# Seven sets of sixteen sequences in the seven-product form instead of five, and the rest in one group of eight, one of two and two of four

## The chip, the cores and the metric

The kernel runs on one core of a Trainium2 chip. Five engines work side by side, each through its own list of instructions in order: TensorE (PE in the profile; PEld is its weight load), VectorE (DVE), ScalarE (ACT), GpSimd (POOL) and SyncE (SP), whose list mostly issues transfers. The metric is device time in microseconds, the median of several runs.

## The reference

There are 128 sequences of 64 tokens with 256 features. Every token goes through two shared networks, and through one of five experts, which a label of its sequence chooses; a small gate on the first token of each sequence weighs the three outputs. The sum is added to x, and a diffusion step over tokens and features follows.

```python
s0 = _dense(x, swi[0], swo[0])                 # relu(x @ wi) @ wo, 256 -> 1024 -> 256
s1 = _dense(x, swi[1], swo[1])
h  = relu(einsum('bsd,bdf->bsf', x, wi[type_label]))
eo = einsum('bsf,bfd->bsd', h, wo[type_label])
w  = softmax(relu(concat(eo[:,0], s0[:,0], s1[:,0]) @ g1) @ g2)
x  = x + eo * w[:,0] + s0 * w[:,1] + s1 * w[:,2]
x  = x + (zX * lap_x + zY * lap_y + zR * x * (1 - x))
```

The labels are drawn from 0, 1 and 2 alone. In the drawn inputs 43 sequences have label 0, 50 have label 1 and 35 have label 2. The kernel learns this only on the chip.

## The kernel before

**Precision.** Every operand of a product is kept as a high and a low part (`split`, L121: ScalarE rounds the value into the high part, another engine, mostly VectorE, subtracts to get the low part). One product is then three matmuls: high by high, high by low, low by high. In the second layer "wide" matmuls of 512 columns hold the high and the low part of the output weights side by side, and "narrow" ones of 256 columns add the low part of the hidden layer.

**Units and slots.** `order_batches` (L261) counts the labels, gives every sequence a slot, and writes a small integer table `tab`: which sequence sits in which slot, which expert each unit of four slots (`NB`) has, and one last number that decides a branch. An expert's sequences are first laid out in sets of sixteen (four units), then the rest of it in pairs of units, then single full units, then what is less than three sequences. `base` holds the ends of these stretches; `base[5]` is the number of slots in sets of sixteen, `base[10]` that in sets of sixteen and pairs. This is a chain of small VectorE operations, called in three pieces behind the second shared item.

**Stages.** The program is one fixed list:

1. Two shared items on the first 1024 tokens (n = 0, 1), which also split the shared weights and store the split parts in DRAM, as `wo_d` (for the second layer) and `wi_d` (for the first).
2. `NQUAD` = 5 items of the expert on units 0 to 19 (n = 100 to 104), one set of sixteen sequences each.
3. `stream` (L1128): nine groups on the rest: pairs of units (8 sequences, 512 columns), among them a half group (two sequences), then single units (4 sequences, 256 columns): units 20-21, 22-23, 24-25, the half group at unit 32, 26-27, 28, 29, 30, 31.
4. A branch (`tc.If`, L1271): if the last number of `tab` is over 128, units 32 to 34 are worked too, each as a single group. The body lies in the program between this place and the next stage; every engine jumps over it or runs through it.
5. The shared items n = 2 to 31 on the other tokens, with the gate (`load_gate`, `gate_shared`, `gate_hidden_s`, ... in n = 2), the sum and the diffusion.

**Items and groups.** An item (L847, `unit` L702) works 1024 tokens in the seven-product form: the first layer of a quarter of the features is 7 products in place of 8, from sums of weight blocks and of token blocks. It has 84 matmuls of 512 columns in the first layer, 64 wide and 64 narrow ones in the second. A group is plain: a pair of units has 48 matmuls of 512 columns in the first layer (`up`, L1030), 32 wide and 32 narrow ones in the second (`down`, L1044); a single unit has 48 of 256 columns, 16 wide and 16 narrow. `stream` walks a group in steps of two features: two `up`, then the `down` of the step before. Each `up` is evacuated by ScalarE into `gh` (high) and by VectorE into `gl` (low); `down` waits for these.

**What else stage 3 carries.** `ahead(g, f)` (L1077) hangs other work on each feature of a group: the loads of the next group (`load_group_w` L439: first a register load of the expert, then four transfers of 512 KB; `load_group_x` L408: 64 KB for each sequence) and the splits of its weights (`split_group_w` L467, tiles `gwr` into `gw`; for the half group `hi` and `ho`). The first two quarters of the shared first-layer weights had been used plain (`plain_units`), so `reload(u)` and `again(u)` load them again (`wsr`), add up the blocks on GpSimd (`sum_wi`, tile `wsum`), split them (tile `wi`) and store them (`keep_wi`, the transfer `wi_d<-wi`). The split second-layer weights come back (`load_wo`, eight of 512 KB), the next tokens come in (`load_x(1)`) and are split, and the first two first-layer parts and one row for the gate are loaded.

**Order.** In items the order of every engine is that of the code. In groups, other than the half group and the first step after it, only TensorE and the transfers keep the code's order (`in_order`, L115); the tile scheduler places the work of the other engines in their lists when the program is built. SyncE's list is one queue: a transfer that waits for its source holds back all behind it. Before the branch ends, each engine signals an event that the others may wait for.

At the very start `NWARM` matmuls on a cleared tile run while the first loads are on their way (L246).

Of the kernel before, what the change touches and what calls it, by code (L numbers as in the profile page):

```python
# [12 lines left out]
ALU = mybir.AluOpType  # L13
# [4 lines left out]
B, S, D, F = 128, 64, 256, 1024  # L18
NE = 5
NF = F // P  # L20
NQ = NF // 2
NB = 4
NU = B // NB + NE * (NB - 1) // NB
NSLOT = NU * NB
NQUAD = (B // NB - 3 * NE + 3) // 4
NPAIR = (B // NB - NE + 2) // 2
NBIG = NPAIR - 2 * NQUAD
NSURE = B // NB + 1 - 2 * NPAIR
HALF = NBIG - 1
UH = 2 * NPAIR + NSURE - 1  # L30
GROUPS = [(2 * NB * g, 2 * NB) for g in range(2 * NQUAD, NPAIR)] + [(u * NB, NB) for u in range(2 * NPAIR, UH)]
GROUPS.insert(HALF, (UH * NB, NB // 2))
NRUN = len(GROUPS)
GROUPS += [(u * NB, NB) for u in range(UH, NU)]
NG = len(GROUPS)
ST = 4
NT = S // ST
# [1 line left out]
N = ST * B  # L39
LAG = 2  # L40
EI = 100
NWARM = 8


A11, A12, A22, S1, S2, S3, S4 = range(7)
# [4 lines left out]
def cond_resid_kernel(ctx: ExitStack, tc: tile.TileContext, xg, xs, xn, itok, z, we, ws, g1, g2, out):  # L50
# [192 lines left out]
    vec.memset(idle, 0.0)  # L243
    for i in range(2):
        pw = seeded(f"pm_idle{i}")
        for _ in range(NWARM // 2):  # L246
            mm(pw, idle[:, :P], idle, True, True)
    it_i = const.tile([P, 1], I32, name="it_i")
    nc.gpsimd.dma_start(it_i, itok)
# [11 lines left out]
    def order_batches():  # L261
# [100 lines left out]
            vec.tensor_tensor(ge[0], ge[0], ge[i], ALU.min)  # L362
        vec.tensor_tensor(tab[:, NSLOT : NSLOT + NU], ge[0], ge[3], ALU.min)

        vec.tensor_scalar(gt[:, 0:1], base[0:1, 4 * NE :], float(-NB), None, ALU.add)
        vec.tensor_tensor(tab[:, NSLOT + NU :], gt[:, 0:1], base[0:1, 3 * NE : 3 * NE + 1], ALU.max)
        yield
        pm3 = psum("pm_perm")
        mm(pm3[0:1, 0:NSLOT], bc, own, True, True)
# [38 lines left out]
    def load_group_x(g):  # L408
        s0, n = GROUPS[g]
        xr = gxr[g] = group_tile(g, [P, n, 2 * S], F32, "gxr")  # L410
        load_batches(s0, n, lambda j: xr[:, j, :])
# [27 lines left out]
    def load_group_w(g):  # L439
        group_expert(g)  # L440
        for h in range(NQ):
            r = own(g, ("raw", h), lambda: slot4(f"gwr{g}_{h}", F32))
            dma(r, we[bass.ds(gval[g], 1), :, 2 * h : 2 * h + 2, :].rearrange("o p f c -> p (o f) c"))
            graw[g, "both", h] = r
            graw[g, 2 * h], graw[g, 2 * h + 1] = r[:, 0, :], r[:, 1, :]

    def load_group(g):
        load_group_w(g)
        load_group_x(g)
# [17 lines left out]
    def split_group_w(g, f):  # L467
        w = own(g, ("w", f), lambda: slot4(f"gw{g}_{f}"))
        split(w[:, 0, :], w[:, 1, :], graw[g, f], vec)
        gw[g, f] = w  # L470
# [4 lines left out]
    def split_half_w(f):  # L475

        h = f // 2
        r = graw[HALF, "both", h]
        if f % 2:
            w = hout[h] = slot4(f"ho{h}").rearrange("p h c -> p (h c)").rearrange("p (f h c) -> p f h c", f=2, h=2)  # L480
            split(w[:, :, 0, :], w[:, :, 1, :], r[:, :, 256:512], vec)
        else:
            if h % 2 == 0:
                for part in range(2):
                    t = slot4(f"hi{h // 2}{part}")
                    hin[h // 2, part] = t.rearrange("p h c -> p (h c)").rearrange("p (f c) -> p f c", f=4)
            hi, lo = (hin[h // 2, part][:, h % 2 * 2 : h % 2 * 2 + 2, :] for part in range(2))
            split(hi, lo, r[:, :, 0:256], vec)
# [588 lines left out]
    def ahead(g, f):  # L1077

        if g >= NRUN:
            return  # L1080
        if f == 0:
            if g == NRUN - 3:
                slots = nc.values_load(
                    tab[0:1, NSLOT + NU : NSLOT + NU + 1], min_val=0, max_val=NSLOT,
                    skip_runtime_bounds_check_because="the table's entries are bounded on the chip",
                )
                total.append(slots)
            if g + 1 < NRUN:
                if g <= NBIG and g != HALF:
                    load_group_w(g + 1)  # L1090
                if g != HALF:
                    load_group_x(g + 1)
            if g < 2:
                reload(g)
            for u in range(3 * g, min(3 * g + 3, 2 * NQ)):
                load_wo(u)
            if g == NRUN - 2:
                load_x(1)
            if g == NRUN - 1:
                load_wi(2, 0)  # L1100
                load_wi(2, 1)
                load_row()
        if f == 5 and g < 2:
            again(g)
        if g + 1 == HALF and f == 4:
            load_group_x(g + 2)
        if f == 6 and (g + 1 == HALF or NBIG <= g < NRUN - 2):
            load_group_w(g + 2)
        if g == 0 and f + FIRST < NF:
            split_group_w(0, f + FIRST)  # L1110
        if g == HALF + 1 and f + 4 < NF:
            split_group_w(g, f + 4)
        if g + 1 < NRUN:
            if f == (0 if g == HALF else 4):
                split_group_x(g + 1)
            if g + 1 == HALF:
                split_half_w(f)
            elif g == HALF + 1:
                for k in ((), (), (0,), (1,), (2, 3), (4, 5), (6,), (7,))[f]:
                    split_group_w(g + 1, k)  # L1120
            elif g != HALF or f < 4:
                split_group_w(g + 1, f)
        elif f < 7:
            if f < 4:
                sum_x(1, T1 + f, gps)
            split_x(1, (B11, B21, T2, T3, T1, T4, B22)[f], vec)
# [37 lines left out]
    def at(k, *work):  # L1164

        return {divmod(k, 4): list(work)}
# [39 lines left out]
    def reload(u):  # L1206
        e, q = divmod(u, NQ)
        load_raw(u, ws[e, :, 2 * q : 2 * q + 2, :])

    def again(u):  # L1210

        sum_wi(u, gps)
        split_wi(u)
        keep_wi(u)
        wip.pop(u)
# [114 lines left out]
    for p in range(1, NP):  # L1330
        ta, tb = 2 * p, 2 * p + 1
        for e in range(2):
            n = 2 * p + e
            parts = [ahead_w(n)]
            if n == 2:
                parts.append(at(0, load_gate, gate_shared))
                parts.append(at(1, gate_hidden_s))
                parts.append(at(4, lambda: load_y(0)))
                parts.append(at(5, step_factors))
                parts.append(at(4, gate_expert))  # L1340
                parts.append(at(6, gate_hidden_e, lambda: load_y(2)))
                parts.append(at(7, lambda: load_sh(0)))
                parts.append(at(8, lambda: load_eo(0)))
                parts.append(at(9, lambda: load_y(3)))
                parts.append(at(10, gate_weights))
                parts.append(sums(0, 11))
                parts.append(at(12, lambda: load_eo(2)))
                parts.append(at(13, lambda: load_y(1)))
                parts.append(at(16, lambda: load_sh(1)))
                parts.append(starts(ta, 17, 0))  # L1350
            elif n == 3:
                parts.append(at(0, lambda: load_eo(3), lambda: load_eo(1)))
                parts.append(sums(1, 1))
                parts.append(starts(tb, 5))
                parts.append(diffusion(0, 7, True, 4))
                parts.append(at(12, lambda: halo(1)))
                parts.append(next_x(2))
            elif n == 4:
                parts.append(at(2, lambda: load_y(4)))
                parts.append(diffusion(1, 0, False))  # L1360
                parts.append(at(6, lambda: load_eo(4)))
                parts.append(diffusion(2, 6))
                parts.append(at(9, lambda: load_y(5)))
                parts.append(at(11, lambda: load_eo(5)))
                parts.append(starts(ta, 14))
                parts.append(starts(tb, 16, 0))
            elif e == 0:
                parts.append(at(0, lambda t=ta: load_y(t), lambda t=ta: load_eo(t)))
                parts.append(at(4, lambda t=tb: load_y(t), lambda t=tb: load_eo(t)))
                parts.append(diffusion(ta - 2, 2))  # L1370
                parts.append(starts(ta, 10))
                parts.append(starts(tb, 13))
            else:
                parts.append(diffusion(ta - 1, 2))
                parts.append(next_x(p + 1))
            if n == 2 * NP - 1:
                parts.append(at(4, lambda: load_last(n)))
                parts.append(at(8, lambda: split_last_w(n)))
                parts.append(at(9, lambda: split_last_x(n)))
                parts.append(at(10, diagonal))  # L1380
                parts.append(at(12, lambda: halo(ta)))
            left = item(n, left, join(*parts))
# [38 lines left out]
```

## Time and profile before

| | us |
|---|---|
| median of 3 runs | 1032.73 |
| lowest, highest | 1032.59, 1033.43 |
| the profiled execution | 1033.12 |
| its span | 1031.1 |
| TensorE busy in the span | 1025.0 |
| VectorE busy | 811.7 |
| ScalarE busy | 572.2 |
| GpSimd busy | 155.5 |

The span is the time from the first to the last instruction on the core; the execution's own time is 2.0 us longer. Lines of the timeline give start and length of an instruction, engine, line, operation, output<-input and, in brackets, how long the engine had been idle and who ended it. A length includes the drain: matmuls of 512 columns have 390 ns of length and follow each other every 228 ns. Times are microseconds from the span's start. Line 93 and line 108 are helpers that record every matmul and every operation of the other engines, so the tiles' names tell the work.

### The profile page before, as it was taken

What the parts mean: (1) busy time and instruction counts of PE and PEld (TensorE: products, weight loads), DVE (VectorE), ACT (ScalarE), POOL (GpSimd) and SP (SyncE); (2) the same over time, 40 slices, a digit from 0 to 9 for tenths busy, and PEclk for the clock granted to TensorE, in tenths of its full rate; (3) what the DMA queues carried; (4) which work ended last, traced back from release to release, by engine and by line L of the source; (5) the groups of instructions that cost most, each with busy time, mean ns of one, the idle gap of its engine ahead of it and who ended that gap; (6) DMA issues with size and microseconds to landing.
All of it is one profiled execution on the core that took longest, in us unless ns stands there. A gap on an engine that the chain in (4) does not pass through costs nothing.

```text
span 1031.1 us, 15580 instructions
## 1 busy us (share of the span) xinstructions
PE 1025.0 (99%) x5385; PEld 878.2 (85%) x5385; DVE 811.7 (79%) x1498; ACT 572.2 (55%) x1077; POOL 155.5 (15%) x165
## 2 busy tenths in 40 slices
PE   9999999999999999999999999999999999999998
PEld 6878888888888889988888888888888888888888
DVE  7998987988768577758988778678688688688778
ACT  6466776676656467543653644455455364365363
POOL 3000000000013011211441220212212202022020
PEclk9999999999999999999999999999999999999999
DMA  6477233331458766464435435334344163253321
GB/s 219 174 271 259 71 109 94 103 123 52 134 168 308 263 221 196 164 228 175 165 126 175 167 106 178 123 123 168 120 162 158 63 229 123 82 189 133 128 77 47
DMA packets 67122, 159.13 MB, mean 154 GB/s; under 512 B 7680, under 2 KB 34688, under 8 KB 67040
## 3 DMA queue, kind: packets, MB, share of 16 engines
q1 hardware_dynamic: 64512, 149.46, 42.3%
q0 software_dynamic: 2384, 8.52, 2.5%
q8 instruction: 43, 0.70, 0.3%
q14 instruction: 39, 0.32, 0.1%
q10 hardware_dynamic: 144, 0.13, 0.0%
HBM read 126.75 MB, written 31.33 MB: 153 GB/s over the span
## 4 chain that ended last, share of the span: by engine, by line
PE 55%; DVE 2%; issue 0%; ACT 0%; DVEq 0%; ACTq 0%
PE acc L93 29%; PE pb L93 11%; PE pa L93 7%; PE pd L93 7%; DVE eq L108 1%; PE pu L93 0%; DVE eb L108 0%; DVE yb L108 0%; PE pgs L93 0%; DVE ea L108 0%; PE gacc L93 0%; PE pge L93 0%; ACT eq L108 0%; DVE lq L108 0%; DVE gh L108 0%
## 5 line engine op out<-in xcount | busy, mean ns | idle before, releaser
L93 PE MATMUL pb<-x,wi 128*128 128x512 f32 x729 | 207.2, 392 | 0.1
L108 ACT ACTIVATE u<-pb 128x512 f32<-128x512 f32 x162 | 96.9, 598 | 114.8 <-PE pb L93 112.7
L93 PEld LDWEIGHTS pb<-x,wi 128*128 128x128 f32 x729 | 130.9, 189 | 23.6 <-ACT u L108 1.2
L93 PE MATMUL pd<-x,wi 128*128 128x512 f32 x486 | 137.9, 392 | 0.3
L93 PE MATMUL pa<-x,wi 128*128 128x512 f32 x486 | 137.1, 390 | 0.4 <-DVEq L1271 0.4
L108 ACT ACTIVATE pb<-pa 128x512 f32<-128x512 f32 x81 | 47.2, 583 | 118.1 <-PE pa L93 117.4
L108 DVE SCALAR_TENSOR_TENSOR yb<-acc,wgt,yb 128x256 f32<-128x256 f32 x216 | 99.3, 482 | 16.0 <-PE acc L93 12.2
L93 PEld LDWEIGHTS pd<-x,wi 128*128 128x128 f32 x486 | 90.8, 188 | 22.3 <-DVE c L108 2.4
L93 PEld LDWEIGHTS pa<-x,wi 128*128 128x128 f32 x486 | 89.8, 188 | 18.7 <-DVEq L1271 0.6
L108 DVE TENSOR_TENSOR c<-pd,u 128x512 f32<-128x512 f32 x81 | 55.9, 690 | 43.3 <-ACT u L108 32.4
L108 POOL TENSOR_TENSOR la<-yb 128x508 f32<-128x508 f32 (+1 forms) x28 | 32.1, 1147 | 260.7 <-ACT yb L108 259.1
L93 PE MATMUL up<-gxh,gw 128*128 128x512 f32 (+1 forms) x256 | 67.7, 337 | 0.0
L93 PE MATMUL acc<-wo,h_6b 128*128 128x256 f32 (+1 forms) x172 | 56.7, 334 | 0.0
L93 PE MATMUL acc<-wo,h_1b 128*128 128x256 f32 (+1 forms) x172 | 56.7, 333 | 0.0
L93 PE MATMUL acc<-wo,h_7b 128*128 128x256 f32 (+1 forms) x172 | 56.7, 333 | 0.0
L93 PE MATMUL gacc<-gw,gh 128*128 128x512 f32 (+1 forms) x256 | 56.6, 363 | 0.0
L93 PE MATMUL acc<-wo,h_2b 128*128 128x256 f32 (+1 forms) x172 | 56.6, 333 | 0.0
L93 PE MATMUL acc<-wo,h_3b 128*128 128x256 f32 (+1 forms) x172 | 56.5, 332 | 0.0
L93 PE MATMUL acc<-wo,h_4b 128*128 128x256 f32 (+1 forms) x172 | 56.5, 332 | 0.0
L93 PE MATMUL acc<-wo,h_5b 128*128 128x256 f32 (+1 forms) x172 | 56.5, 332 | 0.0
L93 PE MATMUL acc<-wo,h_0b 128*128 128x256 f32 (+1 forms) x172 | 56.4, 332 | 0.0
L108 DVE TENSOR_TENSOR pd<-pd,u 128x512 f32<-128x512 f32 x81 | 55.8, 689 | 0.7 <-PE pd L93 0.6
(275 smaller groups left out, 2446.9 us busy)
## 6 DMA issues: line engine op xcount, KB each, us to landing
wi<-wi_d SPq DMA_DIRECT2D x55, 896.0 KB, 4.5
gwr<-we_in SPq DMA_DIRECT2D x32, 512.0 KB, 5.0
wsr<-we_in SPq DMA_DIRECT2D x20, 512.0 KB, 5.0
xr<-xs_in SPq DMA_DIRECT2D x32, 256.0 KB, 5.0
yb<-xn_in SPq DMA_DIRECT2D x16, 512.0 KB, 5.7
wi_d<-wi SPq DMA_DIRECT2D x8, 896.0 KB, 4.5
y_out<-lq SPq DMA_DIRECT2D x27, 256.0 KB, 2.0
xr<-xg_in SPq DMA_DIRECT2D x80, 64.0 KB, 2.0
```

The lines of the kernel that those rows point to most:

```text
L93: nc.tensor.matmul(out_ap, lhsT=lhsT, rhs=rhs, start=start, stop=stop, skip_group_check=True)
L108: ins = call(*args, **kwargs)
```

## The change

`NQUAD` becomes 7: units 20 to 27 become two more items in the seven-product form (n = 105, 106). Behind them stand four groups: the pair of units 28 and 29, the half group at unit 32, and the single units 30 and 31. Since other labels may not give seven sets of sixteen and one pair, the branch's number is raised to 140 when `base[5]` is under 112 or `base[10]` under 120, and the branch's body then works units 20 to 29 as single groups too: 13 groups in place of 3. For the drawn labels `base[5]` is 112, `base[10]` is 120 and the number is 128, so the body is jumped over in both kernels.

All the work that `ahead` hung on nine groups now hangs on four: both reloads and the half group's loads at the first feature of the pair, the two `again` at its features 3 and 6, the loads of unit 30 at its feature 4, those of unit 31 at feature 6 of the half group. The register of the branch is loaded at the first group. `NWARM` is 9. In n = 2, `gate_hidden_s` comes one place later in the unit. The compiled body that is jumped over has 289 instructions on VectorE (69 before), 481 on ScalarE (101), 352 on SyncE (81).

```diff
-NQUAD = (B // NB - 3 * NE + 3) // 4
-NPAIR = (B // NB - NE + 2) // 2
-NBIG = NPAIR - 2 * NQUAD
-NSURE = B // NB + 1 - 2 * NPAIR
-HALF = NBIG - 1
-UH = 2 * NPAIR + NSURE - 1
-GROUPS = [(2 * NB * g, 2 * NB) for g in range(2 * NQUAD, NPAIR)] + [(u * NB, NB) for u in range(2 * NPAIR, UH)]
-GROUPS.insert(HALF, (UH * NB, NB // 2))
+NFOUR = (B // NB - 3 * NE + 3) // 4
+NQUAD = NFOUR + 2
+UPAIR = 4 * NQUAD
+UH = B // NB
+HALF = 1
+GROUPS = [(UPAIR * NB, 2 * NB), (UH * NB, NB // 2)] + [(u * NB, NB) for u in range(UPAIR + 2, UH)]
 NRUN = len(GROUPS)
-GROUPS += [(u * NB, NB) for u in range(UH, NU)]
+GROUPS += [(u * NB, NB) for u in (*range(4 * NFOUR, UPAIR + 2), *range(UH, NU))]
...
-NWARM = 8
+NWARM = 9
...
-        vec.tensor_tensor(tab[:, NSLOT + NU :], gt[:, 0:1], base[0:1, 3 * NE : 3 * NE + 1], ALU.max)
+        vec.tensor_tensor(gt[:, 0:1], gt[:, 0:1], base[0:1, 3 * NE : 3 * NE + 1], ALU.max)
+        for i, u in ((1, UPAIR), (2, UPAIR + 2)):
+            few = gt[:, i : i + 1]
+            vec.tensor_scalar(few, base[0:1, i * NE : i * NE + 1], float(u * NB), float(NSLOT), ALU.is_lt, ALU.mult)
+            vec.tensor_tensor(gt[:, 0:1], gt[:, 0:1], few, ALU.max)
+        vec.tensor_copy(tab[:, NSLOT + NU :], gt[:, 0:1])
...
         if f == 0:
-            if g == NRUN - 3:
+            if g == 0:
                 slots = nc.values_load(
...
-            if g + 1 < NRUN:
-                if g <= NBIG and g != HALF:
-                    load_group_w(g + 1)
-                if g != HALF:
+                load_group(HALF)
+                reload(0)
+                reload(1)
+            elif g != HALF:
+                if g + 1 < NRUN:
                     load_group_x(g + 1)
-            if g < 2:
-                reload(g)
-            for u in range(3 * g, min(3 * g + 3, 2 * NQ)):
+            for u in {0: (0, 1, 2), HALF + 1: (3, 4, 5), NRUN - 1: (6, 7)}.get(g, ()):
                 load_wo(u)
...
-        if f == 5 and g < 2:
-            again(g)
...
+        if g == 0:
+            if f in (3, 6):
+                again(f // 6)
+            if f == 4:
+                load_group(HALF + 1)
+            if f + FIRST < NF:
+                split_group_w(0, f + FIRST)
+            if f == 4:
+                split_group_x(HALF)
+            split_half_w(f)
+            if f == 7:
+                split_group_w(HALF + 1, 0)
+            return
+        if g == HALF:
+            if f == 0:
+                split_group_x(HALF + 1)
+            if f < 4:
+                split_group_w(HALF + 1, 1 + f)
+            if f == 6:
+                load_group_w(HALF + 2)
+            return
+        if f < 3:
+            split_group_w(g, 5 + f)
         if g + 1 < NRUN:
...
-                parts.append(at(1, gate_hidden_s))
+                parts.append(at(2, gate_hidden_s))
```

## The prediction

> **What bounds the kernel now.** I read the page's busy time and chain of waits first, to see whether any engine but TensorE matters.
>
> ```profile
> PE 1025.0 (99%) x5385; PEld 878.2 (85%) x5385; DVE 811.7 (79%) x1498; ACT 572.2 (55%) x1077; POOL 155.5 (15%) x165
> ...
> q8 instruction: 43, 0.70, 0.3%
> q14 instruction: 39, 0.32, 0.1%
> ...
> PE 55%; DVE 2%; issue 0%; ACT 0%; DVEq 0%; ACTq 0%
> ```
>
> TensorE is idle for 1031.1 - 1025.0 = 6.1 us of the span. So time is saved only by fewer or shorter matmuls, and every new gap on TensorE adds in full. The two queue lines (packets, MB, share) are the fetching of instructions; they matter at the jump.
>
> Second, busy time by stretches, cut at the items and groups that change places: two items (n = 103, 104), two pairs, two singles. Columns: stretch, length, PE, PEld, DVE, ACT, POOL busy, granted clock, DMA share, GB/s.
>
> ```profile
> 174.60:216.00 41.40, 41.40 (x214) 35.42 (x213) 35.15 (x75) 28.86 (x59) 1.37 (x1) 1.00 0.34 107
> 216.00:257.30 41.30, 41.30 (x213) 35.35 (x212) 35.05 (x75) 28.82 (x59) 1.37 (x1) 1.00 0.25 79
> 298.80:320.80 22.00, 22.00 (x110) 18.67 (x109) 16.99 (x26) 14.17 (x28) 5.12 (x5) 1.00 0.83 283
> 320.80:342.80 22.00, 22.00 (x113) 18.79 (x112) 15.71 (x26) 12.85 (x26) 5.14 (x5) 1.00 0.88 306
> 392.00:403.40 11.40, 11.40 (x79) 10.54 (x79) 9.35 (x20) 8.19 (x20) 1.30 (x1) 1.00 0.62 190
> 403.40:414.70 11.30, 11.30 (x82) 10.60 (x81) 8.07 (x18) 7.49 (x19) 1.29 (x1) 1.00 0.72 235
> ```
>
> TensorE never stops in them. An item takes 41.35 us for 16 sequences, a pair 22.05 for 8 (its exact ends lie a few hundredths beyond the cut), a single 11.3 for 4. The DMA share is low in the items and 0.6 to 0.9 in the groups: the groups carry the reloads.
>
> Third, the timeline at the places that change, beginning with the chain that loads, splits and stores the shared weights again.
>
> ```profile
> 305.62 0.43 SPq L119 DMA_DIRECT2D wsr<-ws_in  x1
> ...
> 313.09 0.79 POOL L108 TENSOR_TENSOR wsum<-wsr,wsum 128x128 f32<-128x128 f32 x1
> ...
> 313.92 0.63 ACT L108 ACTIVATE wi<-wsum 128x512 fp32r<-128x512 f32 x1 [0.46 <-POOL wsum L108]
> ...
> 315.99 0.33 SPq L119 DMA_DIRECT2D wi_d<-wi  x1
> 316.57 0.33 SPq L119 DMA_DIRECT2D gwr<-we_in  x1
> ```
>
> SyncE issued nothing between the transfers of 308 us and the store at 315.99: the store waited for its tile, and the next `gwr` load stood behind it.
>
> **1. The matmuls: -6.05 us.** Before, units 20 to 27 are three pairs and two singles: 3 x 22.05 + 2 x 11.3 = 88.75 us. After, they are two items: 2 x 41.35 = 82.7. By counts it comes to the same: 24 more matmuls of 512 columns at 0.2275 us from start to start (+5.46), 96 fewer of 256 columns at 0.1195 (-11.47). The expert's items stall nowhere in n = 103 and 104, and the two new ones have the same code.
>
> **2. Five more small operations in n = 1: +0.7 us.** The branch's number takes seven operations in place of two.
>
> ```profile
> 50.99 0.13 DVE L108 TENSOR_SCALAR gt<-base 1x1 f32<-1x1 f32 x1
> 51.16 0.15 DVE L108 TENSOR_TENSOR tab<-gt,base 1x1 int32<-1x1 f32 x1
> 51.24 0.62 DVE L108 TENSOR_TENSOR wi<-wsr,wi 128x256 fp32r<-128x256 f32 x2
> ...
> 52.99 0.68 DVE L108 TENSOR_TENSOR c<-pd,u 128x512 f32<-128x512 f32 x1
> ```
>
> VectorE works without a break from 47 to 58 us. The matmuls into `pd` at 53.72 already come about 0.3 us late because they need `c`, so nothing covers the five. Dependent ones follow each other every 0.17 to 0.2 us, independent ones every 0.1: 0.4 to 0.95, and I take 0.7.
>
> **3. The loads of unit 30, held by the store: +1.7 us.** Let T be the time since the pair's first `up` (298.83 us before). TensorE needs the `gh` of feature 4 for the `down` of features 4 and 5 at T = 16.47. The chain in after: the first `wsr` is issued at T = 1.8, behind the last stores of `eo` (before, those were issued at 299.00, 1.23 long); it lands 4.7 later; the four operations on GpSimd take 2.84, the split on ScalarE 0.63 and on VectorE 0.68, as in the rows above. So SyncE issues the store at about T = 10.8. The four `gwr` loads of unit 30, now at feature 4, stand behind it in the code's order; with the register load between they are issued from T = 11.7 and land 5.0 to 5.6 later, at T = 16.8 (5.0 is the page's median for them, 5.6 that of this stretch). ScalarE's list of the changed kernel has the split of `gwr` (0.52) ahead of the `gh` of features 4 and 5 (0.6), though their `up` are ready; VectorE's low parts stand behind in the same way. TensorE goes on at T = 17.97, plus 0.25 for the second `gh`: 1.7 late. Bounds: 0, if the load lands as fast as the unloaded ones (4.2 us) and the store is a microsecond earlier; 3.5, with the landing of 7.4 that a backlog gave elsewhere in this trace. I take the middle because both parts of it have rows here.
>
> I walked the other waits of the new stage alike (half group's weights, unit 31's, `again` of the second quarter, next tokens, gate's row); each has 1 to 4 us of slack. The transfers needed between T = 1.8 and T = 53 add up to 15.8 MB (weights of units 30 and 31 4.2, `wo` 4.2, `wi_d` and `wi` 3.7, `wsr` 1.05, tokens and the rest 2.7), 310 GB/s, against 283 and 306 in the pairs of before, where nothing waited for them. That is just enough, so it costs nothing here; it is rival D.
>
> **4. The jump over the larger body: +1.5 us.** Before, n = 2 begins thus:
>
> ```profile
> 436.59 0.42 DVE L108 SCALAR_TENSOR_TENSOR gh<-up,gh 128x256 fp32r<-128x256 f32 x1 [0.30 <-ACT gh L108]
> ...
> 437.89 0.50 PE L93 MATMUL pa<-x,wi 128*128 128x512 f32 x1 [0.35 <-DVEq L1271]
> ```
>
> TensorE's first `pa` waits for VectorE's event (DVEq), which follows its jump, 0.88 us after its last operation. The other three engines are not waited for, and each has 2 us or more of slack behind the jump. VectorE jumps over 69 instructions now, 289 in after. TensorE's fetch line, 0.70 MB for 10,770 instructions and loads, is 65 bytes for each, and one packet 16.3 KB; the other line's packets are 8.2 KB, some 126 instructions. So 69 lands in the next block, which the records show being read ahead, and 289 lands two blocks on. If that block must first be fetched, the wait is one short transfer. The shortest from issue to landing in this trace is 1.8 us (`eo_d` stores of 128 KB), 0.33 of it the issuing: about 1.5. Bounds: 0, if the block is held or the target fetched early, and 1.8, one whole transfer. I take 1.5, since the trace knows no shorter transfer and 289 instructions are more than two packets.
>
> The Trainium skill's page "Runtime: NRT & Kernel Launch", section "Instruction fetch mechanics", speaks of blocks of 16 KiB (256 instructions), two of them held, and of a fetch before execution goes on when a taken branch leaves that window. By its block size VectorE's target would still be in the next block, the term 0 and the sum near -3.8. The packets of this trace are half that size on this queue, and I go by them.
>
> **5. The rest: -0.15 us.** A ninth warming matmul (0.43 each in the eight from 1.27 us on) ends at about 5.2 us, where the first real matmul starts at 5.16 after its own wait for ScalarE: 0 to +0.1, taken 0.05. `gate_hidden_s` one place later takes away gaps of 0.1, 0.17 and 0.18 us at 442 to 446 us and adds a wait of about 0.27 for its `u`: -0.45 to +0.1, taken -0.2.
>
> **The sum.** -6.05 + 0.7 + 1.7 + 1.5 + 0.05 - 0.2 = -2.3 us on the profiled execution of 1033.12, which is 1030.8; that execution is 0.4 above the median of its runs, so against 1032.73 the forecast is about 1030.5.
>
> **Rivals.**
> - **B, the jump is free.** For it: TensorE's own jump shows no fetch wait, and VectorE's 0.88 us is short. Against it: two blocks. Price: -3.8, so 1029.0.
> - **C, the load of unit 30 comes in time.** It needs a store 1.5 us earlier, for instance an earlier `wsr` landing. Price with the jump's fetch: -4.0, 1028.8; without, 1027.3.
> - **E, further waits in the short stage.** Several chains have 1 to 2 us of slack that a landing of 7 us in place of 5 uses up; one or two waits of 2 us: 1032 to 1034.
> - **D, slower: the transfers become the bound.** Place: the last loads of the stage, the first-layer parts and the row that n = 2 needs. The stage gives 15.8 MB to 51 us. At 310 GB/s they are just in time; the saving is gone when the rate falls so far that 2.3 us more are needed, that is at 15.8 / 53.3 = 296 GB/s. At 250 GB/s they take 63 us; less what overlaps with n = 2's start, 6 to 9 us late, about 1037. For it: the fastest slice of the page moves 308 GB/s, and queue order makes holes such as the one at 308 to 316 us. Against: the pairs reached 306 with such a hole in them.
> - **F, the branch is taken.** Then 13 groups at 11.3 us run, +147, about 1180. With `base[5]` at 112, `base[10]` at 120 and the number at 128, each exactly on its limit, it isn't.
>
> **Chances.** Forecast 0.45 (its own range 1029.3 to 1031.6), B 0.27, C 0.10, D 0.10, E 0.07, F 0.01. What a measurement of this kernel can tell from no change is 0.2%, 2.07 us, so faster begins below 1030.67. Faster: B and C and a little under half of the forecast's, 0.58. Same: the rest of the forecast's and most of E, 0.31. Slower: D, F, and little else, 0.11. The range: 1027.6 (C at its best, rounded in) to 1033.3 (the upper bounds of steps 3 and 4 with half of E) leaves out D, F and a few hundredths below.
>
> **What would show it.** Right: n = 105 and 106 at 41.35 us without a gap; a gap of 1.7 us on TensorE ahead of the pair's `gacc` of features 4 and 5, with ScalarE idle for about 4 us ahead of a `gw` that a transfer releases; the gap ahead of n = 2's first `pa` grown from 0.35 to nearly 1.9 with VectorE's event as releaser; the gap ahead of `pd` at 54 us grown from 0.3 to 1.0. Wrong: no gap in the pair (C), the old 0.35 at the jump (B), or gaps where `down`, `pa` or `pgs` wait for weights at a DMA share near 0.9 (D).

## The result: 0.4% slower, and the profile after

| | before | after |
|---|---|---|
| median, us (11 executions each) | 1033.18 | 1037.92 |
| lowest to highest | 1032.44 to 1033.70 | 1035.19 to 1042.71 |
| profiled execution | 1033.12 | 1037.92 |
| its span | 1031.1 | 1036.2 |

The ratio is 1.0042, 95% interval 1.0031 to 1.0053. The forecast was 1030.5, faster, with a range up to 1033.3: it is wrong in sign and the time is outside the range. The times of after also spread over 7.5 us, those of before over 1.3.

The page of the changed kernel, busy time first (its lines are numbered two lower than in the kernel before: L91 and L106 are the helpers L93 and L108):

```profile
PE 1021.0 (99%) x5314; PEld 872.8 (84%) x5314; DVE 826.6 (80%) x1555; ACT 581.0 (56%) x1094; POOL 148.0 (14%) x162
...
q14 instruction: 44, 0.36, 0.1%
...
L91 PE MATMUL pa<-x,wi 128*128 128x512 f32 x534 | 150.6, 390 | 2.8 <-DVEq L1282 2.8
```

TensorE works 4 us less, yet the span is 5.1 us longer: it is idle for 15.2 us in place of 6.1. One of the new waits already stands in the third line, 2.8 us ahead of one `pa`.

Where the time went, by the starts of the same matmuls in the two profiled executions (the first matmul of the second layer, the late `pd` of n = 1, the pair's first `up`, n = 2's first `pa`, the last group of matmuls):

| stretch | before, us | after, us | difference | the prediction's terms |
|---|---|---|---|---|
| start to the second layer of n = 0 | 13.74 | 14.01 | +0.27 | +0.05 |
| to `pd` of n = 1 | 39.98 | 40.67 | +0.69 | +0.7 |
| to the first `up` of the groups | 245.11 | 327.80 | +82.69 | +82.7 |
| groups and jump | 139.06 | 61.02 | -78.04 | -88.75 + 1.7 + 1.5 = -85.55 |
| n = 2 to the end | 588.43 | 587.80 | -0.63 | -0.2 |
| sum | | | +4.98 | -2.3 |

The whole error lies in the group stage: without waits it would be 88.75 us shorter, and 10.7 us of them came back, where 3.2 had been forecast. TensorE's timeline shows three gaps (the bracket gives the idle time and who ended it):

```profile
398.74 0.39 PE L91 MATMUL up<-gxh,gw 128*128 128x512 f32 x1
401.20 2.37 PE L91 MATMUL gacc<-gw,gh 128*128 128x512 f32 x8 [2.07 <-ACT gh L106]
...
427.98 0.28 PE L91 MATMUL up<-gxh,gw 128*128 128x256 f32 x1
431.82 2.93 PE L91 MATMUL gacc<-gw,gh 128*128 128x512 f32 x8 [3.56 <-DVE gh L106]
434.54 0.41 PE L91 MATMUL up<-gxh,gw 128*128 128x256 f32 x1
...
439.10 1.56 PE L91 MATMUL gacc<-gw,gh 128*128 128x512 f32 x8
443.50 0.97 PE L91 MATMUL pa<-x,wi 128*128 128x512 f32 x3 [2.84 <-DVEq L1282]
```

**The gap at 401 us** is step 3 of the prediction. SyncE issues the store of the split weights, then unit 30's loads; ScalarE then sits idle until the first of them lands, with `gh` behind it in its list (SyncE, then ScalarE):

```profile
392.85 0.32 SPq L117 DMA_DIRECT2D wi_d<-wi  x1
393.68 2.76 SPq L117 DMA_DIRECT2D gwr<-we_in  x4
```

```profile
400.03 0.63 ACT L106 ACTIVATE gw<-gwr 128x512 fp32r<-128x512 f32 x1 [5.03 <-DMA gwr<-we_in]
400.57 1.55 ACT L106 ACTIVATE gh<-up 128x512 fp32r<-128x512 f32 x3
```

From start to start of TensorE's work it costs 2.2 us, and 0.4 more for the second `gh` within the eight matmuls behind it.

**The gap at 432 us** was not forecast. The `gacc` there needs both parts of `gh` of unit 31's features 0 and 1. ScalarE had the high parts ready by 427 us. The low parts stand in VectorE's list behind three operations that took 1.75 us each in place of 0.68, exactly while GpSimd added up the next tokens (ScalarE, VectorE, GpSimd):

```profile
426.27 0.66 ACT L106 ACTIVATE gh<-up 128x256 fp32r<-128x256 f32 x2
```

```profile
425.71 0.68 DVE L106 TENSOR_TENSOR x<-xr,x 128x512 fp32r<-128x512 f32 x1
426.31 1.78 DVE L106 TENSOR_TENSOR gw<-gwr,gw 128x512 fp32r<-128x512 f32 x1
428.01 1.75 DVE L106 TENSOR_TENSOR x<-xr,x 128x512 fp32r<-128x512 f32 x1
429.68 1.75 DVE L106 TENSOR_TENSOR gw<-gwr,gw 128x512 fp32r<-128x512 f32 x1
431.35 0.74 DVE L106 SCALAR_TENSOR_TENSOR gh<-up,gh 128x256 fp32r<-128x256 f32 x2
```

```profile
426.06 1.48 POOL L106 TENSOR_TENSOR xt<-xr,xr 128x512 f32<-128x512 f32 x1 [7.03 <-DMA eo_d<-ge]
427.62 1.59 POOL L106 TENSOR_TENSOR xt<-xr,xt 128x512 f32<-128x512 f32 x1
429.18 1.71 POOL L106 TENSOR_TENSOR xt<-xr,xr 128x512 f32<-128x512 f32 x1
430.85 1.73 POOL L106 TENSOR_TENSOR xt<-xr,xt 128x512 f32<-128x512 f32 x1
```

The same shapes take 0.68 on VectorE and 1.29 on GpSimd where the other engine is quiet. Three times 1.07 us is 3.2 of the 3.56.

**The matmuls behind that gap ran at half the clock.** By stretches (length, PE, PEld, DVE, ACT, POOL busy, granted clock, DMA share, GB/s):

```profile
431.80:433.00 1.20, 1.18 (x3) 0.99 (x4) 1.20 (x4) 0.93 (x3) 0.77 (x1) 0.50 0.09 33
433.00:434.00 1.00, 1.00 (x5) 0.81 (x4) 1.00 (x3) 0.24 (x1) 0.00 (x0) 0.50 0.62 209
434.00:435.00 1.00, 1.00 (x7) 1.00 (x7) 1.00 (x3) 0.00 (x0) 0.00 (x0) 0.50 0.20 62
435.00:436.00 1.00, 1.00 (x9) 1.00 (x9) 0.22 (x1) 0.26 (x1) 0.00 (x0) 0.91 0.00 0
```

The eight `gacc` took 2.72 us from 431.82 to 434.54 where the same eight take 1.40 at 436.26: some 1.6 us lost, with the first `up` behind them.

**The gap at 443.5 us** is step 4, the jump: 2.84 us in place of 0.35. Together: 2.6 + 3.7 + 1.6 + 2.5 = 10.4 of the 10.7 us.

### The profile page after: what moved, and what is told of

Read it like the earlier page. It is cut to its first block, busy times and chain, and to the rows that moved or that the text cites. A ratio compares the mean times of both kernels' runs of the same rounds, so it can differ in the third digit from the quotient of the medians.

```text
span 1036.2 us, 15395 instructions
## 1 busy us (share of the span) xinstructions
PE 1021.0 (99%) x5314; PEld 872.8 (84%) x5314; DVE 826.6 (80%) x1555; ACT 581.0 (56%) x1094; POOL 148.0 (14%) x162
## 4 chain that ended last, share of the span: by engine, by line
PE 55%; DVE 2%; issue 0%; ACT 0%; DVEq 0%; ACTq 0%
PE acc L91 29%; PE pb L91 11%; PE pd L91 7%; PE pa L91 7%; DVE eq L106 1%; PE pu L91 0%; DVE eb L106 0%; DVE yb L106 0%; DVE ea L106 0%; PE pgs L91 0%; PE gacc L91 0%; PE pge L91 0%; ACT eq L106 0%; DVE lq L106 0%; DVE h_7b L106 0%
## 5 line engine op out<-in xcount | busy, mean ns | idle before, releaser
L91 PE MATMUL pb<-x,wi 128*128 128x512 f32 x801 | 227.5, 392 | 0.4 <-ACT u L106 0.4
L106 ACT ACTIVATE u<-pb 128x512 f32<-128x512 f32 x178 | 106.6, 599 | 119.9 <-PE pb L91 118.4
L91 PEld LDWEIGHTS pb<-x,wi 128*128 128x128 f32 x801 | 143.8, 189 | 26.1 <-ACT u L106 1.7
L91 PE MATMUL pa<-x,wi 128*128 128x512 f32 x534 | 150.6, 390 | 2.8 <-DVEq L1282 2.8
L91 PE MATMUL pd<-x,wi 128*128 128x512 f32 x534 | 151.4, 392 | 0.8 <-DVE c L106 0.7
L106 ACT ACTIVATE pb<-pa 128x512 f32<-128x512 f32 x89 | 51.9, 583 | 123.7 <-PE pa L91 123.0
L91 PEld LDWEIGHTS pd<-x,wi 128*128 128x128 f32 x534 | 99.9, 188 | 24.5 <-DVE c L106 2.6
L91 PEld LDWEIGHTS pa<-x,wi 128*128 128x128 f32 x534 | 98.8, 188 | 22.6 <-DVEq L1282 3.0
L106 DVE SCALAR_TENSOR_TENSOR yb<-acc,wgt,yb 128x256 f32<-128x256 f32 x216 | 99.3, 482 | 15.9 <-PE acc L91 12.2
L106 DVE TENSOR_TENSOR c<-pd,u 128x512 f32<-128x512 f32 x89 | 61.4, 690 | 46.4 <-ACT u L106 35.2
L106 POOL TENSOR_TENSOR la<-yb 128x508 f32<-128x508 f32 (+1 forms) x28 | 32.2, 1150 | 260.5 <-ACT yb L106 259.0
L106 POOL TENSOR_TENSOR x<-xr,x 128x512 fp32r<-128x512 f32 x15 | 20.1, 1340 | 324.6 <-ACT x L106 209.3
L91 PE MATMUL acc<-wo,h_6b 128*128 128x256 f32 (+1 forms) x188 | 62.1, 334 | 0.0
L91 PE MATMUL acc<-wo,h_1b 128*128 128x256 f32 (+1 forms) x188 | 62.1, 334 | 0.0
L91 PE MATMUL acc<-wo,h_7b 128*128 128x256 f32 (+1 forms) x188 | 62.0, 334 | 0.0
L91 PE MATMUL acc<-wo,h_2b 128*128 128x256 f32 (+1 forms) x188 | 62.0, 333 | 0.0
L106 DVE TENSOR_TENSOR pd<-pd,u 128x512 f32<-128x512 f32 x89 | 61.4, 690 | 0.7 <-PE pd L91 0.6
L91 PE MATMUL acc<-wo,h_3b 128*128 128x256 f32 (+1 forms) x188 | 61.9, 333 | 0.0
L91 PE MATMUL acc<-wo,h_4b 128*128 128x256 f32 (+1 forms) x188 | 61.9, 333 | 0.0
L91 PE MATMUL acc<-wo,h_5b 128*128 128x256 f32 (+1 forms) x188 | 61.9, 333 | 0.0
L91 PE MATMUL acc<-wo,h_0b 128*128 128x256 f32 (+1 forms) x188 | 61.8, 332 | 0.0
L91 PE MATMUL acc<-wo,h_5a 128*128 128x256 f32 (+1 forms) x188 | 58.9, 332 | 0.0
```

What stands on the lines that cost most here:

```text
L91: nc.tensor.matmul(out_ap, lhsT=lhsT, rhs=rhs, start=start, stop=stop, skip_group_check=True)
L106: ins = call(*args, **kwargs)
```

## The experiments

The theory behind the first four runs: each gap has a cause of its own (unit 30's loads behind the store, late tokens at 432 us, the jump), and taking the cause away takes its gap away. The main rival was D of the prediction: the transfers are the bound, and a gap that is mended comes back elsewhere. Medians are compared with after's 1037.92; ratios are to the kernel before, run beside each group of four (1033.42 to 1033.46).

### Unit 30's loads ahead of the store (e1_load)

```diff
-            if f in (3, 6):
-                again(f // 6)
-            if f == 4:
+            if f == 3:
                 load_group(HALF + 1)
+            if f in (3, 6):
+                again(f // 6)
```

> The loads of unit 30 are put ahead of the first store of the split weights in the queue (feature 3 in place of 4, before again). Theory (each wait has its own place in the queue): the gap of 2.2 us ahead of the pair's gacc at 401 us goes, with the 0.4 us by which the eight matmuls behind it ran slow; the later gap of 3.7 us and the one of 2.6 us at the branch stay; about 2.6 us faster than the changed kernel, near 1035. Rival (the transfers are the bound of the stage): the wait comes back at the same size at the next load, within 0.5 us of the changed kernel.

Measured: 1033.66 (1032.38 to 1040.08), ratio 1.0014 [0.9999, 1.0029]. The gap at 401 us is gone; one of 0.67 idle is new ahead of the pair's second `gacc`, since in the new list of ScalarE `gh` of feature 3 stands behind splits that wait for the shared weights. The gain is 4.3 us in the median, not 2.6: in the profiled execution, the fastest of the ten, the gap at 432 us shrank too, to two of 0.63 and 0.51. The transfers gave no wait elsewhere, against the rival. In this run VectorE was further ahead of GpSimd, and only one of the three operations met a sum:

```profile
423.56 0.68 DVE L106 TENSOR_TENSOR gw<-gwr,gw 128x512 fp32r<-128x512 f32 x1
424.16 0.68 DVE L106 TENSOR_TENSOR x<-xr,x 128x512 fp32r<-128x512 f32 x1
424.76 1.79 DVE L106 TENSOR_TENSOR gw<-gwr,gw 128x512 fp32r<-128x512 f32 x1
```

```profile
424.22 1.78 POOL L106 TENSOR_TENSOR xt<-xr,xr 128x512 f32<-128x512 f32 x1 [6.79 <-DMA eo_d<-ge]
```

### The tokens earlier (e2_xr)

```diff
-            if g == NRUN - 2:
-                load_x(1)
...
             if f == 6:
                 load_group_w(HALF + 2)
+                load_x(1)
```

> The four loads of the next tokens are issued in the half group, right behind the weights of unit 31, in place of 9 us later behind the stores of the pair, the tokens of unit 31 and three second-layer weights. Theory (late tokens hold the sums on GpSimd, the sums hold the splits, and the splits stand ahead of gh in ScalarE's list): the gap of 3.7 us ahead of the gacc at 432 us goes, and the clock stays at 1.0 behind it, where it was 0.68: 5 us faster than the changed kernel, near 1033. Rival 1 (GpSimd and VectorE hinder each other, operations of 1.7 us in place of 0.7): the gap stays above 1.5 us. Rival 2 (transfers are the bound): another load is late by as much, at n = 2's first weights or row.

Measured: 1039.48 (1037.77 to 1041.83), ratio 1.0067 [1.0050, 1.0084]: slower still, and the theory of late tokens falls. They were issued 8 us earlier and landed 7 us after their issue, by 418 us, but GpSimd began the sums at 425.30, now behind its part of unit 31's tokens, and three operations of VectorE there took 1.43, 1.42 and 1.77 us. Gaps of 1.16 and 0.40 were left at 428 and 431 us. The first gap was 2.73 in this execution, with the clock at 0.50 from 401.4 to 408.2 us behind it.

### A small body (e3_body)

```diff
-GROUPS += [(u * NB, NB) for u in (*range(4 * NFOUR, UPAIR + 2), *range(UH, NU))]
+GROUPS += [(u * NB, NB) for u in range(UH, NU)]
```

> The changed kernel with a branch's body of 3 groups, as before; the groups for other labels are left out, which these labels don't need. Theory (the jump over 289 instructions on VectorE costs a fetch): the gap of 2.8 us ahead of n = 2's first pa falls to the 0.35 of before, 2.5 us faster than the changed kernel, near 1035.5. Rival (the gap comes from the late stage before it, not from the jump): it stays over 2 us.

Measured: 1035.19 (1033.20 to 1039.33), ratio 1.0020 [1.0006, 1.0034], 2.7 us less. The gap ahead of `pa` is 0.35 again, the two others are there as in after (2.11 and 3.56). The second fetch line of the page (q14) has 39 packets here, as in the kernel before, and 44 in after.

### The jump alone, in the kernel before (e4_big_before)

```diff
-GROUPS += [(u * NB, NB) for u in range(UH, NU)]
+GROUPS += [(u * NB, NB) for u in (*range(20, 30), *range(UH, NU))]
```

> The kernel before with a branch's body of 13 groups, nothing else: the jump alone. Theory: a gap of 2.5 us more ahead of n = 2's first pa, 1035.5 against 1033.2, and no other gap. Rival (the fetch was slow only because transfers were piled up in the changed kernel): 1.5 us or less, 1034.7 or below.

Measured: 1037.26 (1035.44 to 1039.46), ratio 1.0045 [1.0028, 1.0062]. TensorE's timeline has one new gap:

```profile
440.57 0.74 PE L93 MATMUL pa<-x,wi 128*128 128x512 f32 x2 [2.93 <-DVEq L1271]
```

So 2.6 us of idle time come from the body's size alone, in a stage with no waits; the transfers of the changed kernel have no part in it. The median rose by 3.8: three of the four executions had a mean granted clock of 0.998 (1 is full speed), and the one at 1.0 is the fastest.

### A hint for VectorE (e5_hint)

```diff
-    tc.mark_branch_hint_location("seldom", "LikelyTaken", (mybir.EngineType.PE,))
+    tc.mark_branch_hint_location("seldom", "LikelyTaken", (mybir.EngineType.PE, mybir.EngineType.DVE))
```

> The changed kernel with a prefetch hint for the branch on VectorE too, where only TensorE had one. Theory (VectorE's jump waits for the fetch of its target): with the block ahead of time the gap of 2.8 us ahead of n = 2's first pa falls to 0.4, 2.5 us faster than the changed kernel, near 1035.3 as with the small body. Rival (the hint comes too early in the program to be held, or another engine's jump is as late): the gap stays at 2.8, or falls only to that of the next late engine, 1 to 2 us.

Measured: 1034.36 (1032.78 to 1039.50), ratio 1.0014 [0.9995, 1.0032], 3.6 us less, with the large body still in place:

```profile
439.60 0.97 PE L91 MATMUL pa<-x,wi 128*128 128x512 f32 x3 [0.38 <-DVEq L1282]
```

The hint for VectorE alone takes the wait away. So what was waited for was the fetch of VectorE's target, and no other engine's jump stood behind it by more than the 0.38 us that are left. Only 2.5 of the 3.6 us are the jump's. In this execution the first gap was 3.47 us, but ahead of unit 31's first `gacc` no gap was left and ahead of its second one of 0.51, though the sums are still on GpSimd: VectorE was further ahead again, and of its operations ahead of unit 31's `gh` one met a sum (1.78 us). So the size of that gap hangs on the moment at which the two engines meet.

### The sums on VectorE (e6_sums_dve)

```diff
-                sum_x(1, T1 + f, gps)
+                sum_x(1, T1 + f, vec)
```

> The changed kernel with the four sums of the next tokens on VectorE, 0.7 us each alone, in place of GpSimd (1.3 alone, 1.5 to 1.7 as measured); the tokens are as late as before. Theory (the late tokens are the main part of the gap of 3.7 us at 432 us): at least 1.5 us of it are left. Rival (the chain on GpSimd and the VectorE operations that it stretches are the main part): 1 us or less is left, and no operation of VectorE takes over 0.8 us there; 3 to 5 us faster than the changed kernel, the slow clock behind it included.

Measured: the gap at 432 us is down to 0.20 idle, the three operations take 0.68 and so do the sums:

```profile
427.07 0.68 DVE L106 TENSOR_TENSOR gw<-gwr,gw 128x512 fp32r<-128x512 f32 x1
427.67 0.68 DVE L106 TENSOR_TENSOR x<-xr,x 128x512 fp32r<-128x512 f32 x1
428.28 0.68 DVE L106 TENSOR_TENSOR gw<-gwr,gw 128x512 fp32r<-128x512 f32 x1
428.88 0.68 DVE L106 TENSOR_TENSOR xt<-xr,xr 128x512 f32<-128x512 f32 x1
```

The rival is right about the cause: GpSimd and VectorE in each other's way. The time is 1037.13 (1034.20 to 1038.73), ratio 1.0034 [1.0023, 1.0045], only 0.8 below after's and not the 3 to 5 us that the rival gave. In the profiled execution the first gap was 2.73 and the one at the jump 2.66, and the clock was 0.50 behind both: the matmuls there took about 1.6 and 1.3 us longer than in after. Why the median gained so little isn't settled. The other two gaps went on drawing the clock down (the median of the mean clocks is 0.997 in both kernels), and the gap at 432 us need not be 3.56 us in every execution of after, by what e5_hint shows.

### How long an idle TensorE costs the clock (e7_gap, e9_gap11, e10_gap16)

```diff
         vec.tensor_tensor(tab[:, NSLOT + NU :], gt[:, 0:1], base[0:1, 3 * NE : 3 * NE + 1], ALU.max)
+        for _ in range(7):
+            vec.tensor_tensor(gt[:, 0:1], gt[:, 0:1], base[0:1, 3 * NE : 3 * NE + 1], ALU.max)
```

The kernel before, with 7, 11 and 16 such operations.

> The kernel before with seven idle small operations behind the branch's number on VectorE in n = 1. Theory on the operations (0.14 us each, nothing covers them): the gap ahead of pd at 54 us grows from 0.3 by 0.14 x 7 to about 1.3 us, 1.0 us slower than before, near 1034.4. Theory on the clock (a gap of some 2 us on TensorE lets the granted clock fall for a few us, a shorter one doesn't): clock 1.0 in all runs, times within 1.5 us of each other. Rival (any gap over 1 us does it): clock 0.998 or lower in some runs and a spread of 3 us or more, as with the gaps of 2.7 us.

> The kernel before with eleven idle small operations in place of seven in n = 1, where no transfer is waited for and nothing jumps: the gap ahead of pd grows to about 2.3 us (0.18 each by the run with seven), TensorE idle for 2.0. Theory (it is TensorE's idle time itself that lowers the clock, and 2 us are enough for some executions): some runs below 1035.6, some up to 4 us above, clock 0.998 or less in these. Rival (the slow clock came from the transfers or the jump around the gaps): all within 1.5 us of 1035.4, clock 0.999 or 1.0.

> The same with sixteen: a gap of about 3.2 us, TensorE idle for 2.9 as at the jump. Theory: as there, most runs show 0.998 or less and lie up to 4 us above the lowest, which is near 1036.2. Rival: all within 1.5 us of 1036.2 at a clock of 1.0.

| operations | TensorE idle, us | median | lowest to highest | executions with a mean clock of 0.998 or less |
|---|---|---|---|---|
| 7 | 1.31 | 1034.06 | 1033.81 to 1034.96 | 0 of 10 |
| 11 | 2.03 | 1035.59 | 1034.59 to 1036.31 | 7 of 10 |
| 16 | 2.94 | 1037.13 | 1036.85 to 1038.70 | 5 of 5 |

An operation costs 0.18 us here, not 0.14: 7 of them widened the gap by 1.28. Idle time alone brings the slow clock, at a place with no jump and no late transfer; 1.3 us didn't, 2.0 did in most executions. None of the 59 executions of the kernel before that ran beside the experiments had a mean clock of 0.998 or less. With eleven, the seven such executions are also the seven slowest; the profiled one is not among them, so only with sixteen is it seen that the clock falls just behind the gap. The stretches behind the gap with sixteen, columns as above:

```profile
56.90:58.00 1.10, 0.99 (x4) 0.86 (x5) 1.10 (x4) 1.01 (x2) 0.00 (x0) 0.92 0.75 313
58.00:59.00 1.00, 1.00 (x3) 0.80 (x3) 1.00 (x4) 0.11 (x1) 0.00 (x0) 0.50 1.11 444
59.00:60.00 1.00, 1.00 (x4) 0.74 (x3) 1.00 (x3) 0.69 (x2) 0.00 (x0) 0.50 0.93 379
60.00:61.00 1.00, 1.00 (x4) 0.81 (x3) 0.97 (x5) 0.90 (x3) 0.00 (x0) 0.50 1.00 397
61.00:62.00 1.00, 1.00 (x5) 0.78 (x5) 1.00 (x3) 0.00 (x0) 0.00 (x0) 0.88 1.12 356
```

The "up to 4 us above the lowest" of the theory was too much for one gap: these spread over 1.7 and 1.9 us. In the median the sixteen cost 3.7 us, 2.9 of it the wider gap. The seven cost 0.6, less than the 1.28 by which their gap widened, so the medians tell such amounts only to some 0.7 us.

### All together (e8_all, e11_all_again, e12_all_third)

The hint, the sums on VectorE, unit 30's loads ahead of the store, eight warming matmuls, and the five small operations moved to the first item of the expert:

```diff
+        yield
+        pm3 = psum("pm_perm")
+        mm(pm3[0:1, 0:NSLOT], bc, own, True, True)
+        vec.tensor_copy(tab[:, 0:NSLOT], pm3[0:1, 0:NSLOT])
+        yield
         for i, u in ((1, UPAIR), (2, UPAIR + 2)):
...
         vec.tensor_copy(tab[:, NSLOT + NU :], gt[:, 0:1])
-        yield
-        pm3 = psum("pm_perm")
-        mm(pm3[0:1, 0:NSLOT], bc, own, True, True)
-        vec.tensor_copy(tab[:, 0:NSLOT], pm3[0:1, 0:NSLOT])
...
+        if n == EI:
+            parts.append(at(8, order))
```

In e8_all the tokens are also loaded early, as in e2_xr. e11_all_again leaves them where the changed kernel has them and puts the first `again` at feature 4, behind unit 30's loads; e12_all_third has it at feature 3.

> All together: unit 30's loads ahead of the store, tokens early, their sums on VectorE, a hint for VectorE, the five operations moved to the first item of the expert, eight warming matmuls. Theory (the gain of 6 us is there once the waits are gone): 1026.5 to 1027.5, clock 1.0, no gap over 0.5 us behind 60 us. Rival (the transfers are the bound of the stage): a gap of 2 us or more between 380 and 460 us whatever the order, 1029 or more.

> As the version with everything together, but the tokens are loaded where the changed kernel has them, and the first again stands one feature later, behind unit 30's loads, so that ScalarE's list has gh of feature 3 ahead of the split that waits for the shared weights. Theory (the gaps of 1.1, 0.6, 1.2 and 0.4 us left in that version come from these two orders): one gap or none over 0.5 us between 380 and 440, 1027.5 to 1029. Rival (the short stage has no room, the gaps move): 1030.5 or more.

> The same, with again where the first try of unit 30's loads had it (feature 3): by the theory the gap of 0.7 to 0.9 us of that run ahead of the pair's second gacc is left and nothing else over 0.5 us, 1028.5 to 1029.5; it tells the two orders apart.

| | median | lowest to highest | ratio to before | gaps left, 380 to 440 us (idle) |
|---|---|---|---|---|
| e8_all | 1030.75 | 1029.85 to 1031.02 | 0.9969 [0.9956, 0.9982] | 0.94, 0.43, 1.18, 0.39 |
| e11_all_again | 1028.84 | 1027.46 to 1029.85 | 0.9956 [0.9939, 0.9973] | 0.20 |
| e12_all_third | 1028.56 | 1027.80 to 1029.36 | 0.9951 [0.9934, 0.9967] | 0.56, 0.93, 0.20 |

e8_all missed its forecast: the time is the rival's (1029 or more), but no gap reaches the rival's 2 us. Moving the tokens early cost more than it gave: e12_all_third, 2.2 us faster, differs from e8_all in that alone. e11_all_again did as its theory said. In e12_all_third the 0.56 us ahead of the second `gacc` was forecast, the 0.93 at 426 us wasn't. e11 and e12 can't be told apart by their times; the trace shows that the later `again` removes the gap ahead of the pair's second `gacc`. Both are faster than the two kernels, by 4.6 and 4.9 us against before. The group stage of e11_all_again in one line:

```profile
380.60:440.00 59.40, 58.78 (x350) 51.36 (x349) 45.60 (x84) 39.36 (x86) 7.96 (x11) 1.00 0.81 302
```

TensorE is busy for 58.78 of 59.4 us while the transfers run at 302 GB/s. So the transfers were not the bound: rival D is out.

## Why the prediction was wrong

- **Step 1, the matmuls: right.** The stretch that holds the two new items grew by 82.69 us against 82.7, and e11_all_again realises 4.6 of the 6.05 us.
- **Step 2, the five operations: right.** +0.69 against +0.7. VectorE's list shows the split that follows `tab` 0.93 us behind the first operation on the number, 0.25 before.
- **Step 3, unit 30's loads behind the store: right in place and chain, taken too small.** It cost 2.6 us with the 0.4 for the second `gh`, against 1.7 with 0.25 of it for that; the upper bound was 3.5. The loads were issued at T = 11.2, half a microsecond earlier than forecast, but ScalarE could begin on the first only 6.3 us after its issue, where the sum had 5.0 to 5.6. e1_load confirms the cause.
- **Step 4, the jump: right in mechanism, mis-sized.** +2.5 us against +1.5, and above the upper bound of 1.8. The shortest transfer in the trace was no bound for a fetch. The runs that show it are e3_body, e4_big_before and e5_hint. The packets of 8.2 KB, by which the prediction chose, pointed the right way. The Trainium skill's page "Runtime: NRT & Kernel Launch", section "Instruction fetch mechanics", gives blocks of 16 KiB; the prediction's estimate from them was a term of 0, which the 2.5 us measured exclude. That the blocks are as small as the packets is not shown by this.
- **"I walked the other waits of the new stage alike ... each has 1 to 4 us of slack": this step failed.** The durations that the prediction shows are those of undisturbed rows (0.63, 0.68). When the stage was squeezed from 139 to 61 us, GpSimd's four sums fell on three VectorE operations ahead of unit 31's `gh`, and these became 1.07 us longer each, 3.2 us together. There was no slack to take them up: without them some 0.4 us of the gap would remain, and e6_sums_dve kept 0.20. What had used up the slack of the walk isn't shown. Rival E allowed for a late landing, and nothing for two engines in each other's way; yet the trace of before had it in sight, as a row of two such operations in 3.07 us beside GpSimd's work (VectorE, GpSimd):

```profile
420.63 3.07 DVE L108 TENSOR_TENSOR x<-xr,x 128x512 fp32r<-128x512 f32 x2 [0.62 <-ACT x L108]
```

```profile
421.41 1.74 POOL L108 TENSOR_TENSOR xt<-xr,xr 128x512 f32<-128x512 f32 x1
423.51 1.35 POOL L108 TENSOR_TENSOR xt<-xr,xt 128x512 f32<-128x512 f32 x1 [0.36 <-POOL xt L108]
```

- **No term for the clock.** The sum added gaps as if TensorE went on at full speed. Two of the gaps that it named, 1.7 and 1.85 us, were near what was enough in the runs (1.31 never was, 2.03 mostly), and the measured ones were all above 2.0. That cost 1.6 us in the profiled execution. Over the eleven executions the mean clock goes from 0.998 in the three fastest to 0.993 in the slowest; 0.005 of some 1040 us is an estimate of 5 of the 7.5 us of spread. The rest isn't explained here; gaps of a different size from one execution to the next would do it.
- **Step 5: small and not settled.** +0.27 for the start against +0.05, but the second layer began between 13.5 and 14.3 us in the runs with eight warming matmuls and between 13.7 and 14.3 in those with nine, so little of it can be put down to the ninth. n = 2 to the end is 0.63 shorter against 0.2; what of it is `gate_hidden_s` wasn't tried alone.
- **Rival D ended on the right side for the wrong reason.** Its price of about 1037 is near the measured 1037.92, which is luck: the time was lost in the stage that it named, but by queue order, two engines, the jump and the clock, not by the rate of transfers. The fastest slice of the page moves 338 GB/s in after, 308 before, so 310 was no ceiling.

## What to carry to other kernels

When a stage is squeezed, walk its waits with the durations that its operations have beside their new neighbours: look in the trace for the same shape running long, and see which engine ran at that moment. Expect a gap on TensorE of 2 us or more to cost more than its length in many executions, and take such gaps away together, since one removed among three may not show in the median. A branch's body that is never run still has a price, which is read from the engine whose event the next stage waits for, and a hint for that engine can take it away.

## What the runs showed of the hardware

- **VectorE and GpSimd slow each other.** An operation on 128 x 512 with two inputs took 0.68 us alone and 1.4 to 1.8 beside a GpSimd sum, and that sum 1.29 alone and 1.5 to 1.8. The Trainium skill's page "SBUF — State Buffer", section "Who interferes with whom", says that a VectorE `tensor_tensor` with both inputs in SBUF contends with GpSimd's reads, since VectorE's second input comes through the read interface that the two share. The traces agree that the two slow each other.
- **An idle TensorE can lose its clock after some 2 us.** After 2.03 us idle the mean clock was 0.998 or less in 7 of 10 executions, after 2.94 in 5 of 5, after 1.31 in none of 10. Not every such gap does it: 2.94 us at the jump in the profiled execution of e1_load left the clock at 1.00. Where it fell, it was 0.50 for 3.4 us (431.8 to 435.2 in the changed kernel, 57.8 to 61.2 with sixteen operations), once for 6.8 us (e2_xr). The page "TensorE: Matmul & The Clock Gate", section "HAM oscillation — how this bites in real kernels", gives as a rule no idle gaps over about 3.4 us; here shorter ones were enough. That only some executions fall may fit the free-running window of which the same page speaks in "What's actually happening", but no run here tests that.
- **A jump over 289 instructions cost VectorE 2.5 us more than one over 69,** and a hint for VectorE took all of it away: the wait ahead of `pa` is 0.35 us before, 2.84 after, 2.93 in e4_big_before and 0.38 in e5_hint. Whether the number of instructions decides, or the place of the target in a block, no run separates.
